# Row loads and folded steps moved to other cycles in the first pass of a two-layer graph attention kernel

## The chip, the cores and the metric

The kernel runs on one core of one Trainium2 chip. The metric is the device time of one execution in microseconds. An engine is called by its short name: PE is TensorE (the matrix engine), DVE is VectorE, ACT is ScalarE, POOL is GpSimd and SP is SyncE, which here only asks for DMA transfers. A profiled execution gives a span, from the first to the last recorded instruction, and a time of its own, which is a little longer.

## What is computed

The input `x` has 4096 rows of 512, `adj` is a 4096 x 4096 matrix of zeros and ones. Two layers follow each other, each with a residual and a layer norm. The first is graph attention with eight heads of 64 columns, and all that matters here lies in it:

```python
feats  = einsum('nf,hfo->hno', X, W)
s_self = einsum('hno,ho->hn', feats, a_self)
s_neigh = einsum('hno,ho->hn', feats, a_neigh)
dense = s_self[:, :, None] + s_neigh[:, None, :]
dense = where(dense > 0, dense, 0.2 * dense) * A[None, :, :]
out = einsum('hij,hjo->hio', softmax(dense, axis=-1), feats) + b[:, None, :]
x = layernorm(x + relu(out))
```

The second layer is attention inside 32 graphs of 128 rows, with scores that are shifted by the adjacency:

```python
a = where(mask, query @ key.T * scale, 0.0)
scores = (a + adj + adj) * where(mask, 1.0, -1000000.0)
x = layernorm(x + (softmax(scores, axis=-1) * mask) @ value)
```

## The kernel before

**Passes, chunks, steps and cycles.** The eight heads are taken in four passes `r` of two heads each. A pass goes through four chunks `c` of 1024 columns (C), and a chunk through 32 steps `j` of 128 neighbours. In passes 0 to 2 (called the first to third) eight steps make a cycle (`wide=8`), so a chunk has four cycles; in the last pass a cycle has four steps, and the second layer's work is threaded between them by a plan that is written out by hand. The instructions of PE stand in the order of the program; a scheduler orders those of the other engines, except for those that `in_order` pins to program order.

**What a step does.** The exponential of a leaky ReLU is a product of a row factor and the larger of two terms. So DVE makes, for each of the two heads, `q = max(p_row, d) * at` (L1534), in which `at` is the turned adjacency block of 128 x 1024. ACT, or DVE for one of eight, makes `mark` from q (L1544, L1539): which side of the maximum was taken. PE multiplies: `accf` gets f_s times at (L1558, four products of 512 columns a step, called the A products), `acc` gets g_s times q (L1581, eight products of 32 rows a step, which the profile counts as sixteen), and `dens` gets the marks (L1597). In the first pass `ae` also gets sums over the adjacency (L1479).

**A folded step** leaves its four A products out. DVE forms `q = (max(p_row, d) * U_row - c) * at` with two operations for each head in place of one (L1522 and L1525), and the L1581 products of that step go to `accf`. `folded(j)` says which steps of a pass do so, in the first and in the last pass only. The U rows lie in two tiles of the pool `ck`, loaded once a chunk (`rows_for_folded`, L1462), which are free again when the last folded step of the chunk before has read them.

**Where the adjacency comes from.** In the first pass POOL asks for a block of it (`load_adjacency`, L605: 1024 x 512 numbers, four steps, made fp8 on the way; the pool has three of them, `a_b`). PE turns it (`turned_steps`, L617), ACT casts it into `at` (`cast_steps`, L628), and POOL writes `at` to `at_d` in DRAM (L629), from where SP reads it back in the later passes (L635). A cycle turns the steps of the next cycle: four after the A products and four after the sums over the adjacency. They are called the first and the second turn. The request for the block of step j + 10 is pinned at the turn of j, wherever j % 4 is 2; so the block that is asked for at a second turn is used at the first turn of the next cycle but one, about a cycle and the A products later.

**The rows of a chunk.** `p_row` (two tiles of 512 KB, two buffers each) is needed from a chunk's first step on. `u_row` (two halves of 256 KB, one buffer) is needed at the end of the chunk alone, where `sums_to_rows` makes `ys = (accf + S) * u_row` and adds `acc` (L1278, L1286); what is left of that function, with `n0` and `hst` (L1306, L1312, L1362) and the write of the chunk's rows to `hs_d` (L1372), runs in the next chunk's first three cycles. [...] f_s (512 KB for four steps) and g_s (256 KB) have two buffers each, so those of the next cycle are asked for as PE finishes with those of this one.

Of the kernel before, what the change touches and what calls it, by code (L numbers as in the profile page):

```python
# [10 lines left out]
F32 = mybir.dt.float32  # L11
# [8 lines left out]
P = 128  # L20
# [378 lines left out]
def broadcast_rows(v, parts, n):  # L399

    return bass.AP(tensor=v.tensor, offset=v.offset, ap=[[0, parts], [1, n]])
# [3 lines left out]
def adjacency_streamed_path(  # L405
# [29 lines left out]
    nc = tc.nc  # L435
    N, F = x.shape
    H, _, FH = W.shape
    NT = N // P
    FC = F // P
    PR = H // 2  # L440
    FP = 2 * FH
# [3 lines left out]
    C = 1024  # L445
    CT = C // P
    NCH = N // C
# [14 lines left out]
    g_d = dram.tile([PR, NT // 4, P, 4 * FP], F32, name="g_d")  # L462
    f_d = dram.tile([PR, NT // 4, P, 4 * 2 * FP], F32, name="f_d")
    FOLDED = (0, PR - 1)
    FOLDS = {4: (1,), 5: (0, 1), 6: (0, 1, 2)}, {2: (1,), 4: (1,), 5: (0, 1), 6: (0, 1, 2)}
    HU = 2 * len(FOLDED)
    pu_d = dram.tile([2 * H + HU, N], F32, name="pu_d")
    at_d = dram.tile([NCH, NT, P, C], F32, name="at_d")
# [73 lines left out]
    rowp = ctx.enter_context(tc.tile_pool(name="rows_f", bufs=2))  # L542
    urowp = ctx.enter_context(tc.tile_pool(name="urows", bufs=1))
# [46 lines left out]
    def in_order(pinned, ins):  # L590

        if pinned:
            tc.keep_in_program_order(ins)
# [29 lines left out]
    def cast_steps(c, j, pt, steps=range(2)):  # L623

        both = pt.rearrange("p t n -> p (t n)").bitcast(FP8).rearrange("p (n k) -> p n k", k=2)
        for k in steps:
            at = ats[0, c, j + k] = ring("at", atp, 6).tile([P, C], F32R, name="at")
            ends_of_setup["ACT"] = nc.scalar.copy(at, both[:, :, k])  # L628
            nc.gpsimd.dma_start(at_d[c, j + k], at.bitcast(F32))  # L629
# [9 lines left out]
    with tc.tile_pool(name="setup1", bufs=1, side="right") as one, tc.tile_pool(  # L639
        name="setup_rows", bufs=1, side="right"  # L640
    ) as late, tc.tile_pool(name="setup2", bufs=2, side="right") as two, tc.tile_pool(
        name="xtp", bufs=4, side="right"
    ) as xtp, tc.tile_pool(name="staged1", bufs=1, side="right") as staged1, tc.tile_pool(
        name="staged2", bufs=2, side="right"
    ) as staged2, tc.tile_pool(
        name="ps_setup", bufs=3, space=PSUM
    ) as pss, tc.tile_pool(name="ps_feat", bufs=2, space=PSUM) as psf:
        NB = NT // 4
        xts, xTs, pu_js, rows = {}, {}, {}, {}
# [773 lines left out]

    steps = [(r, c, j) for r in range(PR) for c in range(NCH) for j in range(NT)]

    def main_pass(r, ae=None, wide=4):

        for c in range(NCH):
            p_row = []
            for h in range(2):  # L1430
                p_row.append(rowp.tile([P, C], F32, name=f"p_row{h}"))
                in_order(
                    r == 0 and c < 2,
                    nc.sync.dma_start(p_row[h], broadcast_rows(pu_d[2 * r + h, ts(c, C)], P, C)),
                )
            u_row = urowp.tile([P, C], F32, name="u_row")
            for h in range(2):
                in_order(
                    r == 0 and c < 2,
                    nc.sync.dma_start(  # L1440
                        u_row[h * FH : (h + 1) * FH, :],
                        broadcast_rows(pu_d[H + 2 * r + h, ts(c, C)], FH, C),
                    ),
                )
            U_row = []

            def folded(j):

                if r == PR - 1:
                    return r in FOLDED and c > 0 and j % 4 in FOLDS[c > 1].get(j // 4, ())  # L1450
                return r in FOLDED and j % 8 == 2 and (0 if c else 8) < j < NT - 8

            def rows_for_folded():

# [35 lines left out]
            for j0 in range(0, NT, wide):  # L1490
                at_step = steps.index((r, c, j0))
                cycle = range(j0, j0 + wide)
                f_s, g_s = {}, {}
                for k in range(j0 // 4, (j0 + wide) // 4):
                    f_s[k] = fsp.tile([P, 4, 2, FP], F32R, name="f_s")
                    ins = nc.sync.dma_start(
                        f_s[k].rearrange("p u s n -> p (u s n)").bitcast(F32), f_d[r, k]
                    )
                    in_order(r == 0 and c == 0 and j0 < 16, ins)
                    g_s[k] = gfp.tile([P, 4, 2, FH], F32, name="g_s")  # L1500
                    ins = nc.sync.dma_start(
                        g_s[k].rearrange("p u h o -> p (u h o)"), g_d[r, k]
                    )
                    in_order(r == 0 and c == 0 and j0 < 16, ins)
                if at_step == 0:
                    cast_steps(0, 6, last_pair)
                if any(map(folded, range(NT))) and j0 == (4 if r else 0):
                    rows_for_folded()
# [6 lines left out]
                for j in cycle:  # L1515
                    for h in range(2):
# [3 lines left out]
                        if folded(j):  # L1520
                            cn = c_all[r][:, j, h : h + 1]
                            nc.vector.scalar_tensor_tensor(  # L1522
                                q, p_row[h], d_j, U_row[h], op0=OP.max, op1=OP.mult
                            )
                            nc.vector.scalar_tensor_tensor(  # L1525
                                q, q, cn, ats[r, c, j].bitcast(F32), op0=OP.subtract, op1=OP.mult
                            )
                            mark = marks[j, h] = sgp.tile([P, C], FP8, name="mark")
                            nc.scalar.activation(  # L1529
                                mark, q, AF.Sigmoid, bias=below_0, scale=2.0**80, saturate=False  # L1530
                            )
                            continue
# [5 lines left out]
                        if j % 4 == 3 and h == 1:  # L1538
                            nc.vector.tensor_scalar(  # L1539
                                mark, q, d_j, None, op0=OP.is_gt, saturate=False  # L1540
# [14 lines left out]
                for j in cycle:  # L1555
                    for w in range(0 if folded(j) else 2):
                        for s in range(2):
                            nc.tensor.matmul(  # L1558
                                accf[:, s, :],
                                f_s[j // 4][:, j % 4, w, :],  # L1560
                                ats[r, c, j][:, ts(s, HB)],
                                start=(j == 0 and w == 0),
                                stop=(j == NT - 1 and w == 1),
                            )
# [11 lines left out]
                for j in cycle:  # L1576
                    dst = accf if folded(j) else acc
                    for s in range(2):
                        for o in range(0, FP, 32):
                            h = o // FH  # L1580
# [47 lines left out]
    with tc.tile_pool(name="ps_ae", bufs=1, space=PSUM) as psx:  # L1628
        ae = psx.tile([P, HB], F32, name="ae")
        nc.vector.memset(ae, 0.0)  # L1630
        banks.append(psx)
        main_pass(0, ae, wide=8)
        banks.remove(psx)
    first_pass.close()
    banks.extend([ctx.enter_context(tc.tile_pool(name="ps_misc2", bufs=2, space=PSUM))] * 2)
    with tc.tile_pool(name="wl1", bufs=1, side="right") as wp:
        work.append(weights_of_layer_1(keep, wp))
        work.append(kind_of_graphs(wp))
        work.append(kind_of_scores(wp))
        main_pass(1, wide=8)  # L1640
        for gen in work:
            for _ in gen:
                pass
        work.clear()
    main_pass(2, wide=8)
    more.clear()
    wide_passes.close()
    with tc.tile_pool(name="lp", bufs=2) as lp, tc.tile_pool(
        name="lp1", bufs=1
# [7 lines left out]
@with_exitstack  # L1657
def tile_gat_then_graph_attention(ctx: ExitStack, tc: tile.TileContext, *args: bass.AP):
    nc = tc.nc
    keep = ctx.enter_context(tc.tile_pool(name="flag", bufs=1))  # L1660
    flag = keep.tile([1, 1], I32, name="flag")
    adjacency_streamed_path(tc, flag, *args)
    other = nc.values_load(flag[0:1, 0:1], min_val=0, max_val=1)
    with tc.If(other > 0):
        general_path(tc, *args)
# [42 lines left out]
```

## Time and profile before

| | us |
|---|---|
| median of three runs | 2042.51 (2039.18 to 2042.93) |
| the profiled execution's own time | 2043.19 |
| its span | 2041.3 |
| PE busy | 2005.9 |
| DVE busy | 1744.8 |
| ACT busy | 1533.1 |
| first pass on PE, from the first A product | 160.2 to about 582 |

In the views below, a row of a timeline has the start in us, the duration in us, the engine, the line, the operation, what is written from what, the shape, and how many instructions were merged into it; in brackets stands how long the engine sat idle before, and what ended that. A row of SPq is a request, not the transfer. The strip called DMA has 40 equal slices of the span, each with the share of time in tenths that the DMA engines were busy.

### The profile page before, as it was taken

The page shows a single profiled execution, that of the slowest core. Times are in us where ns is not written, and L with a number is a line of the kernel's source. Part 1 is how long each engine was busy: PE and PEld are TensorE (multiplying, and loading weights), DVE is VectorE, ACT ScalarE, POOL GpSimd, SP SyncE. Part 2 cuts the span into 40 slices and gives each one's busy share as a digit, 9 for nine tenths or more (in the row PEclk, how much of TensorE's full clock was granted, in tenths as well). Part 3 has the DMA queues.
Part 4 walks back from the last instruction along what each step waited for, and adds up shares of the span by engine and source line. Part 5 has one row for each costly group of instructions (what it writes and reads, how often), then busy time and mean ns, then how long its engine had stood idle before and what let it go on. Part 6 is the DMA issues. An engine that isn't in the chain of part 4 may idle for free.

```text
span 2041.3 us, 38200 instructions
## 1 busy us (share of the span) xinstructions
PE 2005.9 (98%) x14981; PEld 1030.0 (50%) x14981; DVE 1744.8 (85%) x2219; ACT 1533.1 (75%) x1872; POOL 231.0 (11%) x362
## 2 busy tenths in 40 slices
PE   8999999999999999999999999999999999999997
PEld 7885545444444444444444544444444444445443
DVE  5668898898999998798999989999997897889754
ACT  3348988788888889788899889999786566567420
POOL 1222222222200000000000000000020210211111
PEclk9999999999999999999999999999999999999999
DMA  6899999999999999788999999989975775775211
GB/s 206 240 320 280 283 286 288 285 280 282 316 377 342 346 359 342 261 311 292 318 321 338 313 328 338 335 277 368 323 277 186 249 255 173 232 273 176 73 55 44
DMA packets 209386, 558.70 MB, mean 274 GB/s; under 512 B 25052, under 2 KB 66012, under 8 KB 209196
## 3 DMA queue, kind: packets, MB, share of 16 engines
q1 hardware_dynamic: 144844, 433.65, 61.0%
q0 software_dynamic: 62272, 121.98, 23.3%
q8 instruction: 120, 1.97, 0.4%
q10 hardware_dynamic: 2080, 0.52, 0.1%
q14 instruction: 70, 0.57, 0.1%
HBM read 499.13 MB, written 107.28 MB: 297 GB/s over the span
## 4 chain that ended last, share of the span: by engine, by line
PE 85%; DMA 7%; DVE 5%; issue 1%; ACT 1%; SPq 0%; POOL 0%; POOLq 0%; DVEq 0%; ACTq 0%
PE acc L1581 35%; PE accf L1558 20%; PE ps_fe L818 5%; PE ps_m L1186 5%; PE ps_m L1114 5%; PE dens L1597 5%; DMA a_b<-in_adj_dram 4%; DVE q L1534 3%; PE accf L1581 2%; PE ps_m L1141 1%; PE ps_m L1200 1%; DMA hp_l<-hs_d 1%; PE ps_m L617 1%; DMA at_d<-at 1%; PE ps_m L1043 1%
## 5 line engine op out<-in xcount | busy, mean ns | idle before, releaser
L1534 DVE SCALAR_TENSOR_TENSOR q<-p_row,d_all,at 128x1024 f32<-128x1024 f32 x962 | 1168.1, 1279 | 106.0 <-PE acc L1581 78.8
L1544 ACT ACTIVATE mark<-q,nb_all 128x1024 fp8e4<-128x1024 f32 x834 | 926.8, 1144 | 174.7 <-DVE q L1534 160.1
L1581 PE MATMUL acc<-q,g_s 128*32 128x512 f32 x7696 | 853.7, 594 | 1.1 <-DVE q L1534 0.4
L1581 PEld LDWEIGHTS acc<-q,g_s 128*32 128x32 f32 x7696 | 250.2, 110 | 557.2 <-issue 496.3
L1558 PE MATMUL accf<-at,f_s 128*128 128x512 f32 x1924 | 469.3, 400 | 1.7 <-ACT at L628 1.6
L1558 PEld LDWEIGHTS accf<-at,f_s 128*128 128x128 f32 x1924 | 357.2, 189 | 107.3 <-issue 27.8
L1249 ACT ACTIVATE ck<-ck,neg_half_f 128x1024 f32<-128x1024 f32 x128 | 146.0, 1141 | 28.5 <-DMA ck<-in_adj_dram 28.4
L1250 ACT ACTIVATE ck<-ck,neg_quarter 128x1024 f32<-128x1024 f32 x128 | 146.3, 1143 | 1.8
L1597 PE MATMUL dens<-mark,e_b 128*6 128x512 fp8e4 x2048 | 125.3, 379 | 2.5 <-DVE mark L1539 2.5
L818 PE MATMUL ps_fe<-w_sb_f,xT_f 128*128 128x264 f32 (+1 forms) x512 | 121.6, 395 | 1.7 <-ACT xT_f L730 1.7
L628 ACT CAST at<-ps_m 128x1024 fp32r<-128x1024 fp8e4 x124 | 116.3, 1022 | 4.8 <-issue 2.0
L1186 PE MATMUL ps_m<-wvT,x1T 128*128 128x512 f32 x256 | 114.2, 594 | 0.0
L1114 PE MATMUL ps_m<-x1T,M_sb 128*128 128x512 f32 x256 | 113.1, 595 | 0.0
L818 PEld LDWEIGHTS ps_fe<-w_sb_f,xT_f 128*128 128x128 f32 x512 | 100.5, 200 | 16.2 <-ACT xT_f L730 2.3
L1372 POOL DMA_DIRECT2D hs_d<-hst x12 | 10.7, 896 | 828.1 <-DVE hst L1362 817.5
L1539 DVE TENSOR_SCALAR mark<-q,d_all 128x1024 fp8e4<-128x1024 f32 x128 | 96.2, 751 | 4.7
L629 POOL DMA_DIRECT2D at_d<-at x128 | 69.1, 540 | 272.5 <-ACT at L628 94.0
L1597 PEld LDWEIGHTS <-e_b 128*6 128x6 bf16 x2048 | 55.9, 86 | 80.1 <-issue 38.2
L1529 ACT ACTIVATE mark<-q,below 128x1024 fp8e4<-128x1024 f32 x62 | 69.6, 1153 | 24.5 <-DVE q L1525 24.2
L1114 PEld LDWEIGHTS ps_m<-x1T,M_sb 128*128 128x128 f32 x256 | 48.0, 190 | 58.9 <-issue 57.1
L1525 DVE SCALAR_TENSOR_TENSOR q<-q,c_all,at 128x1024 f32<-128x1024 f32 x62 | 77.3, 1273 | 0.0
L1186 PEld LDWEIGHTS ps_m<-wvT,x1T 128*128 128x128 f32 x256 | 47.7, 190 | 56.3 <-issue 55.1
(207 smaller groups left out, 1294.9 us busy)
## 6 DMA issues: line engine op xcount, KB each, us to landing
at<-at_d SPq DMA_DIRECT2D x384, 512.0 KB, 6.1
f_s<-f_d SPq DMA_DIRECT2D x128, 512.0 KB, 7.8
at_d<-at POOLq DMA_DIRECT2D x128, 512.0 KB, 19.1
ck<-in_adj_dram SPq DMA_DIRECT2D x128, 512.0 KB, 5.5
g_s<-g_d SPq DMA_DIRECT2D x128, 256.0 KB, 5.9
f_d<-fst POOLq DMA_DIRECT2D x16, 1024.0 KB, 7.5
a_b<-in_adj_dram POOLq DMA_DIRECT2D x32, 512.0 KB, 21.7
p_row<-pu_d SPq DMA_DIRECT2D x32, 512.0 KB, 6.7
```

Of the source, the lines that this page charges most:

```text
L628: ends_of_setup["ACT"] = nc.scalar.copy(at, both[:, :, k])
L818: nc.tensor.matmul(pf[:, q, :, cols], tile_j(xTs[k][:, c].rearrange("p u n -> p (u n)"), u), w_sb[:, c, 4 * q : 4 * q + 4, cols], start=(c ...
L1114: nc.tensor.matmul(pz, L1["M"][:, f, ts(c, P)], x1T[:, f, :], start=(f == 0), stop=(f == FC - 1),)
L1186: nc.tensor.matmul(pv, x1T[:, f, ts(u, P)], L1["wvT"][:, f, :], start=(f == 0), stop=(f == FC - 1),)
L1249: tc.keep_in_program_order(nc.scalar.activation(ck, ck, AF.Square, bias=neg_half))
L1250: nc.scalar.activation(ck, ck, AF.Abs, bias=neg_quarter, accum_out=binp[:, k : k + 1])
L1534: ends_of_setup["Q"] = nc.vector.scalar_tensor_tensor(q, p_row[h], d_j, ats[r, c, j].bitcast(F32), op0=OP.max, op1=OP.mult)
L1539: nc.vector.tensor_scalar(mark, q, d_j, None, op0=OP.is_gt, saturate=False)
L1544: nc.scalar.activation(mark, q, AF.Sigmoid, bias=nb_all[:, j, hh : hh + 1], scale=BIG, saturate=False,)
L1558: nc.tensor.matmul(accf[:, s, :], f_s[j // 4][:, j % 4, w, :], ats[r, c, j][:, ts(s, HB)], start=(j == 0 and w == 0), stop=(j == NT - 1 an ...
L1581: nc.tensor.matmul(dst[o : o + 32, s, :], g_s[j // 4][:, j % 4, h, o % FH : o % FH + 32], qs[j, h][:, ts(s, HB)], start=(j == 0), stop=(j ...
L1597: nc.tensor.matmul(dens[lo : lo + 6, :], e_b[:, j, 2 * r + h, :], marks[j, h][:, ts(s, HB)], start=(j == 0), stop=(j == NT - 1),)
```

## The change

In the first pass the folded steps are 8, 16 and 24 of every chunk. They were 10 and 18 in chunk 0 and 2, 10 and 18 in the others. The two halves of `u_row` are asked for with a chunk's second cycle instead of its start (chunk 0 keeps it at the start), and the next chunk's `p_row` with the third cycle. Both are pinned on SP's queue. The load of `f_s` leaves out the folded steps at the two ends of its four, in both passes that fold. The table `FOLDS` is written by chunk, with the same steps as before.

```diff
-    FOLDS = {4: (1,), 5: (0, 1), 6: (0, 1, 2)}, {2: (1,), 4: (1,), 5: (0, 1), 6: (0, 1, 2)}
+    FOLDS = {1: {4: (1,), 5: (0, 1), 6: (0, 1, 2)}, 2: {2: (1,), 4: (1,), 5: (0, 1), 6: (0, 1, 2)}, 3: {2: (1,), 4: (1,), 5: (0, 1), 6: (0, 1, 2)}}
...
+    p_rows = {}
+
+    def load_p_rows(r, c, pinned):
+
+        rows = []
+        for h in range(2):
+            rows.append(rowp.tile([P, C], F32, name=f"p_row{h}"))
+            ins = nc.sync.dma_start(rows[h], broadcast_rows(pu_d[2 * r + h, ts(c, C)], P, C))
+            in_order(pinned, ins)
+        return rows
+
+    def load_u_row(r, c, pinned):
+
+        u_row = urowp.tile([P, C], F32, name="u_row")
+        for h in range(2):
+            ins = nc.sync.dma_start(
+                u_row[h * FH : (h + 1) * FH, :],
+                broadcast_rows(pu_d[H + 2 * r + h, ts(c, C)], FH, C),
+            )
+            in_order(pinned, ins)
+        return u_row
...
         for c in range(NCH):
-            p_row = []
-            for h in range(2):
-                p_row.append(rowp.tile([P, C], F32, name=f"p_row{h}"))
-                in_order(
-                    r == 0 and c < 2,
-                    nc.sync.dma_start(p_row[h], broadcast_rows(pu_d[2 * r + h, ts(c, C)], P, C)),
-                )
-            u_row = urowp.tile([P, C], F32, name="u_row")
...
+            p_row = p_rows.pop((r, c), None) or load_p_rows(r, c, (r, c) == (0, 0))
+            if r or c == 0:
+                u_row = load_u_row(r, c, r == 0)
...
-                return r in FOLDED and j % 8 == 2 and (0 if c else 8) < j < NT - 8
+                return r in FOLDED and j % 8 == 0 and j > 0
...
+                    live = [u for u in range(4) if not folded(4 * k + u)]
                     ins = nc.sync.dma_start(
-                        f_s[k].rearrange("p u s n -> p (u s n)").bitcast(F32), f_d[r, k]
+                        f_s[k][:, live[0] : live[-1] + 1].rearrange("p u s n -> p (u s n)").bitcast(F32),
+                        f_d[r, k, :, live[0] * 2 * FP : (live[-1] + 1) * 2 * FP],
                     )
...
+                if r == 0 and c and j0 == 8:
+                    u_row = load_u_row(r, c, True)
+                if r == 0 and c < NCH - 1 and j0 == 16:
+                    p_rows[r, c + 1] = load_p_rows(r, c + 1, True)
```

More of the change, by code (lines that the diff above doesn't have):

```diff
@@ L1424, in adjacency_streamed_path @@
     steps = [(r, c, j) for r in range(PR) for c in range(NCH) for j in range(NT)]
+    p_rows = {}
[15 more added lines that the diff above has]
+        return u_row
     def main_pass(r, ae=None, wide=4):
         for c in range(NCH):
-            p_row = []
-            for h in range(2):
-                p_row.append(rowp.tile([P, C], F32, name=f"p_row{h}"))
-                in_order(
-                    r == 0 and c < 2,
-                    nc.sync.dma_start(p_row[h], broadcast_rows(pu_d[2 * r + h, ts(c, C)], P, C)),
-                )
-            u_row = urowp.tile([P, C], F32, name="u_row")
[L1437 to L1444, printed above, removed]
+            p_row = p_rows.pop((r, c), None) or load_p_rows(r, c, (r, c) == (0, 0))
+            if r or c == 0:
+                u_row = load_u_row(r, c, r == 0)
             U_row = []
@@ L1449, in folded @@
                 if r == PR - 1:
-                    return r in FOLDED and c > 0 and j % 4 in FOLDS[c > 1].get(j // 4, ())
-                return r in FOLDED and j % 8 == 2 and (0 if c else 8) < j < NT - 8
+                    return r in FOLDED and c > 0 and j % 4 in FOLDS[c].get(j // 4, ())
+                return r in FOLDED and j % 8 == 0 and j > 0
             def rows_for_folded():
```

## The prediction

> **What bounds the kernel now.** I read the page's busy times first, then TensorE's timeline over the first pass, then what stands behind each of its gaps on the queues.
>
> ```profile
> PE 2005.9 (98%) x14981; PEld 1030.0 (50%) x14981; DVE 1744.8 (85%) x2219; ACT 1533.1 (75%) x1872; POOL 231.0 (11%) x362
> DMA  6899999999999999788999999989975775775211
> ```
>
> TensorE is busy 98% of the span; slices 3 to 16 (100 to 810 us) also have every DMA engine busy 90% or more. The first pass runs from 160.2 to 582 us. A cycle of eight steps there is: A products into accf, first turn (L617), 128 products into acc, dens, ae, second turn. Without a wait A takes 6.5 us to the next turn with one folded step and 7.4 without. The timeline at three starts of a chunk:
>
> ```profile
> 264.86 6.97 PE L1558 MATMUL accf<-at,f_s 128*128 128x512 f32 x28
> 272.24 1.07 PE L617 MATMUL ps_m<-ident_b,a_b 128*128 128x128 bf16 x16 [0.41 <-DMA a_b<-in_adj_dram]
> ...
> 369.24 7.01 PE L1558 MATMUL accf<-at,f_s 128*128 128x512 f32 x28
> 379.89 1.07 PE L617 MATMUL ps_m<-ident_b,a_b 128*128 128x128 bf16 x16 [3.63 <-DMA a_b<-in_adj_dram]
> 380.88 5.31 PE L1581 MATMUL acc<-q,g_s 128*32 128x512 f32 x32
> ...
> 478.58 7.00 PE L1558 MATMUL accf<-at,f_s 128*128 128x512 f32 x28
> 487.78 1.07 PE L617 MATMUL ps_m<-ident_b,a_b 128*128 128x128 bf16 x16 [2.19 <-DMA a_b<-in_adj_dram]
> 488.78 3.64 PE L1581 MATMUL acc<-q,g_s 128*32 128x512 f32 x32
> ```
>
> From the start of A to the turn are 7.38, 10.65 and 9.20 us; less 6.53 that is 0.85, 4.12 and 2.67, together **7.64 us** of waiting for a block of the adjacency. After the longest, 32 products take 5.31 instead of 3.64: 1.67 us more. So **9.3 us** lie at three starts. A wait of L617 for DVE later in each of these cycles (0.35 to 0.37 us shown) is left alone by the change.
>
> The late block is the one that POOL asks for at 352.91. Its row in POOL's timeline, and SP's rows just then:
>
> ```profile
> 348.51 0.91 POOL L1372 DMA_DIRECT2D hs_d<-hst  x1 [5.27 <-DVE q L1534]
> 352.91 0.90 POOL L605 DMA_DIRECT2D a_b<-in_adj_dram  x1 [1.17 <-DMA at_d<-at]
> ```
> ```profile
> 352.38 1.09 SPq L1440 DMA_DIRECT2D u_row<-pu_d  x2
> 362.38 1.51 SPq L1434 DMA_DIRECT2D p_row<-pu_d  x2
> ```
>
> It lands 26.9 us later; those of 244.15 and 461.25 take 28.0 and 26.5; elsewhere it is 17.9 to 25.4. All three share their flight with u_row (2 x 256 KB) and p_row (2 x 512 KB). POOL's writes at_d take 17 to 25 us to land (medians of the DMA view, cycle by cycle): its queue has a standing backlog.
>
> [...] the three blocks in flight with SP's rows are the slowest. [...] the DMA view of 552 to 576 us has 408 GB/s, which I use. [...] Here 3.63 us idle cost 1.67 us and 2.19 us cost nothing[...].
>
> **The change, part by part.** A cycle's DMA work, with a_b counted as read (four bytes for each written), is 8 x 0.524 for at_d, 2 x 2.10 for a_b and 1.57 MB for f_s and g_s: 9.96 MB, or 24.4 us at 408 GB/s, beside 25 to 26 us of TensorE. Row loads (p, u, and U rows in ck: 2.62 MB) and hs_d (0.52) add 7.7 us to a chunk. An estimate: 105 us of DMA, where chunk 1 took TensorE 104.4 (264.86 to 369.24) with 0.85 of waiting. DMA and TensorE are level, and DMA falls behind where rows bunch.
>
> 1. Folded steps: 12 for 11. Per chunk they were 2, 3, 3, 3 and are 3 each, now at steps 8, 16 and 24. One more fold takes four A products away; A's two lengths in the timeline (7.58 and 6.68) give 0.9 us: **-0.9 us**, on the path. It costs DVE two operations, 2.5 us, in chunk 0's last cycle; in chunk 1's DVE waited 2.16 and 1.54 us there (<-PE), so it is free. If that cover were gone, up to +2.5.
> 2. The folds leave the first cycle, where DVE also has the chunk's two ys operations (1.28 and 1.22). DVE loses 2.5 us there and gains it in the fourth cycle, which had none. In DVE's order as many operations stand ahead of n0 (L1306) and hst (L1362) as before, so hs_d is asked for no later. On the path: 0.
> 3. Rows. SP asked at a chunk's start for u and the next-but-one p; now u is asked for with the second cycle and the next p with the third. U rows (ck) wait for the last fold and move from the start of the third cycle to its end. u and p are used long after they land (a whole cycle and more), so their own lateness costs 0. On SP the second g_s load of a first cycle no longer stands behind u_row, which waited for ys; a g_s of the fourth cycle now stands behind a ck that waits for DVE's fold, but is needed a cycle later: 0.
> 4. f_s of a block with a folded step 0 is 384 KB, not 512: twelve times in the first pass, 1.57 MB. In the last pass six loads shrink to 256 or 128 KB (three each, 1.97 MB); no wait of TensorE there names f_s, so 0, with half a microsecond either way.
> 5. What rows and f_s give back. DMA never idles from 185 us to the third wait, so a block lands earlier by the work no longer ahead of it. Ahead of each late block one u and one p set are gone (1.57 MB, 3.9 us), and 3, 6 and 9 smaller f_s (0.39, 0.79, 1.18 MB: 1.0, 1.9, 2.9 us): 4.8, 5.8 and 6.7 us. Without waits TensorE would arrive 0.85, 4.97 and 9.3 us earlier (the last with the clock). The first two waits go wholly; at the third, the block is 6.7 us earlier and TensorE could be 9.3, so about 2.6 us of waiting stays: **-6.7 us**. Counting only what is in flight with the block (1.57 MB becomes 1.05 MB of ck, with smaller f_s, 1.6 us a block) gives 0.85 + 1.6 + 1.67 + 1.6 = 5.7. Both ends: 0 (waits move) to 9.3 (all gone). I take 6.7.
> 6. ACT's order changes, which the diff doesn't show: the two marks of a folded step now stand ahead of the four casts (L628) that follow the second turn, and one cast after the first turn stands behind some five marks. In the third cycle of chunk 1 the casts ended 0.6 us before A reached their steps; with DVE's last operation of the fold where a q now ends (343.2), its mark ending at 344.4 and casts 0.95 us apart I get 0.8 us. Cost 0 to +1.4 a cycle (two marks of 1.15 less 0.85); I take 0.
>
> Sum: -0.9 - 6.7 = **-7.6 us**. The profiled execution took 2043.19 us (span 2041.3), so **2035.6**; that execution is 0.7 above the median of 2042.51. Passes 2 to 4 have almost no TensorE waits and should only start earlier. POOL's order is the same.
>
> **Rivals.** *Waits that move (0.24).* p now comes in the third cycle and ck at its end, 2.1 MB just ahead of the very block that was late, whose issue already waits for at_d landings. Then it is no earlier, and only the first wait, the fold and part of the clock come back: 0.9 + 0.85 + 1 = 2.8, about 2040.4. For it: POOL's wait of 1.17 above, and at_d landings of 20 to 25 us after ck loads. Against: 1.57 MB net is gone from ahead of it. *Casts late (0.11, slower).* Place: ACT, after the second turn of each cycle. If DVE's second operation of the fold ends over 0.8 us later than I have it, A waits for at; at the bound of 1.4 us in 12 cycles, 17 us are lost against 7.6 gained: 2052. It turns slower than before from 0.63 us a cycle. *All waits gone (inside the forecast, less likely):* 10.2 us, 2033. *The change doing less than it says:* the built order of SP shows u, p and f_s where I have them, so I give it nothing of its own.
>
> **How the numbers follow.** The forecast (gains of 5 to 10.5) has 0.65, moved waits 0.24, late casts 0.11. About 0.2% (4.1 us) is what a measurement of this kernel can tell from no change. Faster by more: 0.65 and a little of the second case, less gains that fall short: 0.66. Within: 0.23. Slower: 0.11. The forecast's own range is 2032 to 2038; to hold 8 in 10 it reaches over moved waits to 2042, and half a microsecond below for runs under the median.
>
> **What would show it.** Right: L617 at the starts of chunks 1 and 2 without a wait for a_b, under 3 us at chunk 3; no 5.31 after it; a_b landings there of 20 to 24 us; TensorE reaching the second pass 7 to 8 us earlier, and no more gained after it. Wrong: a_b waits of the old size there or new ones inside a chunk (rows); waits of A for ACT's at (casts); a changed time between 582 us and the end.

## The result, and the profile after

| | before | after |
|---|---|---|
| median, us | 2041.64 (12 runs, 2037.71 to 2045.53) | 2035.55 (12 runs, 2030.43 to 2039.35) |
| ratio after / before | | 0.9969, interval 0.9959 to 0.998 |
| profiled execution's own time | 2043.19 | 2035.39 |
| its span | 2041.3 | 2033.6 |
| first pass on TensorE, first A product to the first of the second pass | 422.8 (160.17 to 582.97) | 414.7 (158.71 to 573.43) |

By the ratio the kernel is 6.3 us faster (2.0 to 4.1 parts in a thousand, so 4 to 8 us), by the two medians 6.1; the forecast was 7.6 us faster and 2035.6. A second comparison of the same two kernels, later, gave 0.9964 (0.995 to 0.9977).

The lines of the page of after that answer to those shown of before, the busy times and the strip of the DMA engines in 40 slices:

```profile
PE 2005.0 (99%) x14977; PEld 1027.5 (51%) x14977; DVE 1746.3 (86%) x2221; ACT 1523.3 (75%) x1872; POOL 231.3 (11%) x362
DMA  6999999999999999798999999979976775775211
```

They hardly move: TensorE 99% instead of 98%, the DMA engines still at 9 through the whole first pass. The whole change is in what these lines can't show, the waits. TensorE's timeline of after at the same three starts of a chunk (start, duration, engine, line, operation, shape, count; a wait would stand in brackets):

```profile
262.85 7.57 PE L1573 MATMUL accf<-at,f_s 128*128 128x512 f32 x32
270.26 1.07 PE L617 MATMUL ps_m<-ident_b,a_b 128*128 128x128 bf16 x16
...
367.00 7.60 PE L1573 MATMUL accf<-at,f_s 128*128 128x512 f32 x32
374.44 1.07 PE L617 MATMUL ps_m<-ident_b,a_b 128*128 128x128 bf16 x16
...
471.07 7.56 PE L1573 MATMUL accf<-at,f_s 128*128 128x512 f32 x32
478.54 1.07 PE L617 MATMUL ps_m<-ident_b,a_b 128*128 128x128 bf16 x16
479.54 5.79 PE L1596 MATMUL acc<-q,g_s 128*32 128x512 f32 x52
```

32 A products stand where 28 stood (no folded step in the first cycle any more), and none of the three first turns waits for a block. From the start of A to the turn it is 7.41, 7.44 and 7.47 us, the plain length of 32 products. After the third, 52 products take 5.79 us; the clock granted from 479.5 to 485.3 us is 1.00. The list of waits has the same news in one line each. Before, then after (what waited, for what: us in all, times, the longest):

```profile
PE ps_m L617 <- DMA a_b<-in_adj_dram: 6.2, 3, 3.6
...
PE accf L1558 <- ACT at L628: 1.6, 1, 1.6
```

```profile
PE accf L1573 <- ACT at L628: 2.2, 4, 1.6
```

The first line is gone. The second has grown from one wait to four: the long one, at the start of the pass, is in both, and A now waits for ACT's casts three times more, about 0.2 us each. POOL's timeline of after around the block that was latest before, and SP's requests ahead of it:

```profile
344.46 0.91 POOL L1372 DMA_DIRECT2D hs_d<-hst  x1 [7.28 <-DMA a_b<-in_adj_dram]
346.63 0.54 POOL L629 DMA_DIRECT2D at_d<-at  x1 [1.26 <-ACT at L628]
347.90 0.53 POOL L629 DMA_DIRECT2D at_d<-at  x1 [0.72 <-ACT at L628]
349.18 0.90 POOL L605 DMA_DIRECT2D a_b<-in_adj_dram  x1 [0.75 <-PE accf L1573]
```

```profile
285.63 2.41 SPq L1441 DMA_DIRECT2D u_row<-pu_d  x2
...
311.83 2.61 SPq L1433 DMA_DIRECT2D p_row<-pu_d  x2
...
336.02 0.32 SPq L1471 DMA_DIRECT2D ck<-pu_d  x1
...
339.08 0.32 SPq L1471 DMA_DIRECT2D ck<-pu_d  x1
```

The last rows of u and p ahead of the request at 349.18 were asked for 64 and 37 us before it; the U rows alone stand just ahead. Request and landing of the three late blocks, and the turn that needs each:

| block | before | after | turn of after | in hand |
|---|---|---|---|---|
| chunk 1 | 244.2 + 28.0 | 244.1 + 20.9 | 270.26 | 5.3 |
| chunk 2 | 352.9 + 26.9 | 349.2 + 21.0 | 374.44 | 4.2 |
| chunk 3 | 461.2 + 26.5 | 455.5 + 23.0 | 478.54 | 0.0 |

The last column shrinks from chunk to chunk. DMA is still the slower of the two; the pass ends about when nothing is left in hand.

A single profile scatters outside the first pass: over the kernels run here its start lies between 157.2 and 160.9 us, and what follows it took 1455.3 to 1460.5 us. Before has 160.2 and 1458.3, after 158.7 and 1460.2. So the comparison of two profiles below is made by the length of the first pass, and the comparison of times by medians.

### The profile page after: what moved, and what is told of

The parts are those of the page before. It is cut to its first block, busy times and chain, and to the rows that moved or that the text cites. A ratio compares the mean times of both kernels' runs of the same rounds, so it can differ in the third digit from the quotient of the medians.

```text
span 2033.6 us, 38136 instructions
## 1 busy us (share of the span) xinstructions
PE 2005.0 (99%) x14977; PEld 1027.5 (51%) x14977; DVE 1746.3 (86%) x2221; ACT 1523.3 (75%) x1872; POOL 231.3 (11%) x362
## 5 line engine op out<-in xcount | busy, mean ns | idle before, releaser
L1559 ACT ACTIVATE mark<-q,nb_all 128x1024 fp8e4<-128x1024 f32 x832 | 915.2, 1148 | 140.9 <-DVE q L1549 130.3
```

Of the source, the lines that this page charges most:

```text
L1559: nc.scalar.activation(mark, q, AF.Sigmoid, bias=nb_all[:, j, hh : hh + 1], scale=BIG, saturate=False,)
```

## The experiments

Twelve kernels ran, four at a time, each beside runs of before (medians 2039.8, 2040.4 and 2040.44). Two things had to be told apart: whether the gain comes from DMA work that no longer stands ahead of the late blocks, and which part of the change brings it: the rows, the folds or f_s. "Pass" is the length of the first pass in the one profiled execution.

**1. Rows alone** (`rows_only`: after, with the folds and the f_s of before).

```diff
-                return r in FOLDED and j % 8 == 0 and j > 0
+                return r in FOLDED and j % 8 == 2 and (0 if c else 8) < j < NT - 8
...
-                        f_s[k][:, live[0] : live[-1] + 1].rearrange("p u s n -> p (u s n)").bitcast(F32),
-                        f_d[r, k, :, live[0] * 2 * FP : (live[-1] + 1) * 2 * FP],
+                        f_s[k].rearrange("p u s n -> p (u s n)").bitcast(F32), f_d[r, k]
```

> The u and p requests in the second and third cycle, with the folded steps and the f_s loads of before. Theory (a late block lands earlier by all the DMA work that no longer stands ahead of it): 1.57 MB less ahead of each late block, 3.9 us at 408 GB/s; the wait at chunk 1 (0.85 us) goes, at chunk 2 about 1 us stays and the slow clock after it goes, at chunk 3 some 3 to 4 us in all stay; 3 to 5 us faster than before. Rival (the waits go because DVE has no fold at a chunk's start): the three waits for a_b stay within 1 us of 0.85, 4.12 and 2.67, and the time is that of before.

Measured: ratio 1.0001 (0.9992 to 1.001), pass 419.4. Its timeline has no wait at chunks 1 and 2 and this at chunk 3:

```profile
471.37 7.01 PE L1571 MATMUL accf<-at,f_s 128*128 128x512 f32 x28
481.57 1.54 PE L617 MATMUL ps_m<-ident_b,a_b 128*128 128x128 bf16 x16 [3.19 <-DMA a_b<-in_adj_dram]
483.04 4.79 PE L1594 MATMUL acc<-q,g_s 128*32 128x512 f32 x32
```

The first two waits are gone, as step 5 of the prediction has it, but at chunk 3 a longer one than before is left: 3.19 us, and the products after it are slower (4.79 us where 3.64 is usual). The expected 3 to 5 us did not come: moving the rows alone gives nothing that the times can tell.

**2. Folds alone** (`folds_only`: before, with the folds of after).

```diff
-                return r in FOLDED and j % 8 == 2 and (0 if c else 8) < j < NT - 8
+                return r in FOLDED and j % 8 == 0 and j > 0
```

> Folded steps 8, 16 and 24 of each chunk, with the row requests at the chunk's start and full f_s loads as before. Theory: one more fold gives 0.9 us, DVE's share of the first cycle wins nothing, the three waits for a_b stay (7 to 10 us with the slow clock, perhaps more, since the U rows now come just ahead of u and p): 0 to 1 us faster, or up to 3 us slower. Rival (DVE at the chunk's start): the waits go and it is 8 to 10 us faster.

Measured: 1.0004 (0.9997 to 1.0011), pass 422.0. The waits of its first two chunk starts, in its timeline:

```profile
270.05 1.07 PE L617 MATMUL ps_m<-ident_b,a_b 128*128 128x128 bf16 x16 [0.96 <-DMA a_b<-in_adj_dram]
...
377.95 1.89 PE L617 MATMUL ps_m<-ident_b,a_b 128*128 128x128 bf16 x16 [3.64 <-DMA a_b<-in_adj_dram]
```

The late blocks are as late as before (241.0 + 29.0, 350.6 + 27.3). Chunk 3 had no wait here: the cycle with the wait at chunk 2 took 33.4 us, where 27.0 is its length without one, so TensorE came 6.4 us later to what follows.

**3. All but the smaller f_s** (`full_f`: after, with f_s whole as in experiment 1).

> The changed kernel with every f_s load of 512 KB. Theory: 0.39, 0.79 and 1.18 MB more stand ahead of the three late blocks, 1.0, 1.9 and 2.9 us; in the changed kernel these land about 5.3, 4.2 and 0.0 us ahead of the turn that needs them, so only the third turn waits, by about 2.9 us: 2 to 3 us slower than the changed kernel, 4.5 to 5.5 us faster than before. Rival (only what is in flight with the block counts, 0.13 to 0.26 MB): under 0.7 us, so 7 to 8 us faster than before.

Measured: 0.9978 (0.9971 to 0.9984), pass 415.4. One wait for a block is left, at chunk 3:

```profile
479.65 1.07 PE L617 MATMUL ps_m<-ident_b,a_b 128*128 128x128 bf16 x16 [0.76 <-DMA a_b<-in_adj_dram]
```

So rows and folds together bring 4.5 us, though neither brings any alone. Without the smaller f_s the block of chunk 3 lands at 479.6 instead of 478.5. About 2.9 us of waiting were expected there, and under 0.7 by the rival; the 0.76 stand by the rival.

**4. p one cycle later** (`p_fourth`).

```diff
-                if r == 0 and c < NCH - 1 and j0 == 16:
+                if r == 0 and c < NCH - 1 and j0 == 24:
```

> The changed kernel with the next chunk's p asked for with the fourth cycle instead of the third: the same work ahead of the late block, but now in flight with it. Theory (all work ahead counts): the same landings and the same time as the changed kernel, within 1 us. Rival (what is in flight counts): the late blocks take 2.6 us longer to land (1.05 MB), and with 5.3, 4.2 and 0.0 us in hand the turn at chunk 3 waits about 2.6 us.

Measured: 0.9978 (0.9972 to 0.9985), pass 415.3. p is again in flight with the late blocks, which take 22.9, 24.6 and 26.5 us to land for 20.9, 21.0 and 23.0 of after, and still TensorE waits only 0.36 us at chunk 3:

```profile
481.16 1.07 PE L617 MATMUL ps_m<-ident_b,a_b 128*128 128x128 bf16 x16 [0.36 <-DMA a_b<-in_adj_dram]
```

The rival had 2.6 us. At chunks 1 and 2 the time in hand takes the slower landing up. At chunk 3, where there is none, the block was asked for earlier: 18.6 us ahead of the chunk's first A product for 15.6 in after. So work counts that lies ahead of a block, whether it flies with the block or delays its request.

**5. Folds in the third step of a cycle** (`fold_26`: full_f, with folds 10, 18 and 26). It is meant to take the casts' lateness away and nothing else.

```diff
-                return r in FOLDED and j % 8 == 0 and j > 0
+                return r in FOLDED and j % 8 == 2 and j > 8
```

> Rows asked for as in the changed kernel, full f_s loads, folded steps 10, 18 and 26 of every chunk: out of a chunk's first cycle, but third in their cycle, so that ACT's marks stand behind the four casts after the second turn as before. Two theories. If what counts is that the first cycle has no fold (its first turn then comes 0.9 us later, 7.4 instead of 6.5 us after the first A product, and DVE has less to do there), this is as good as the changed kernel with full f_s (4.5 us faster than before) or better, and the A products lose their 0.1 to 0.5 us a cycle of waiting for casts: 5 to 8 us faster than before. If the folded step must be first in its cycle, it is like the rows alone: within 2 us of before.

Measured: 0.9988 (0.9981 to 0.9995), pass 420.2. A no longer waits for casts (fourth cycles 24.9 us instead of 25.3 to 25.4), but blocks are late again, one of them at a third cycle. Its timeline at both places:

```profile
427.44 1.07 PE L617 MATMUL ps_m<-ident_b,a_b 128*128 128x128 bf16 x16 [2.47 <-DMA a_b<-in_adj_dram]
428.44 3.64 PE L1594 MATMUL acc<-q,g_s 128*32 128x512 f32 x32
...
483.07 1.21 PE L617 MATMUL ps_m<-ident_b,a_b 128*128 128x128 bf16 x16 [3.64 <-DMA a_b<-in_adj_dram]
484.20 6.00 PE L1594 MATMUL acc<-q,g_s 128*32 128x512 f32 x40
```

TensorE's own work is shorter here than in full_f, and the kernel isn't faster (its median stands 2.6 us below before, full_f's 4.9, in different sets of runs). The expected 5 to 8 us did not come. In this profile the two waits cost 8.2 us where TensorE's own work is 2 us shorter, and the execution lies 2.4 us over its kernel's median; the intervals of the two ratios overlap. So the waits can come back here; that they always cost what the shorter work gains is not shown.

**6. Folds in the fifth step** (`fold4`: after, with folds 12, 20 and 28).

```diff
-                return r in FOLDED and j % 8 == 0 and j > 0
+                return r in FOLDED and j % 8 == 4 and j > 4
```

> The changed kernel with folded steps 12, 20 and 28: the fifth of their cycle, in the second half of it, f_s loads still shrunk (its last three steps). The casts that A waited for now have four whole steps of A products before them, so the waits of A for at should go (about 2 us over the pass): 6 to 9 us faster than before. Rival: the fold now falls into the acc products, where DVE is only just ahead of TensorE (2.5 us for a step's two q against 1.73), so acc waits 1 to 2.5 us in each of 12 cycles: 10 us slower than that or more.

Measured: 1.0078 (1.0065 to 1.0092), pass 437.3. No block is late; cycles are 27.0 to 28.1 us instead of 25.3 to 27.1. Its groups on TensorE's weight loads, and its DVE timeline at a chunk's first fold:

```profile
L1596 PEld LDWEIGHTS acc<-q,g_s 128*32 128x32 f32 x900 | 29.9, 109 | 72.6 <-issue 51.0 <-DVE q L1549 18.9 <-DVE q L1537 1.8
```

```profile
360.72 2.48 DVE L1537 SCALAR_TENSOR_TENSOR q<-p_row,d_all,ck 128x1024 f32<-128x1024 f32 x2 [2.97 <-PE acc L1596]
363.12 2.47 DVE L1540 SCALAR_TENSOR_TENSOR q<-q,c_all,at 128x1024 f32<-128x1024 f32 x2
```

In the stretch from 265 to 480 us those loads wait 20.7 us for a q of DVE; in after it is 4.8. DVE first stands idle until products of acc are done, then has four operations to do where two are usual, and q is late. With TensorE about 2 us slower in all cycles but a chunk's first, every block lands more than 11 us ahead of its turn. So the place of a fold within its cycle decides over some 16 us against before.

**7. No rows** (`no_rows`: before, with p and u loaded in chunk 0 alone in the first pass).

```diff
-            p_row = []
-            for h in range(2):
+            if r or c == 0:
+                p_row = []
+            for h in range(2) if r or c == 0 else ():
...
-            u_row = urowp.tile([P, C], F32, name="u_row")
-            for h in range(2):
+            if r or c == 0:
+                u_row = urowp.tile([P, C], F32, name="u_row")
+            for h in range(2) if r or c == 0 else ():
```

> The kernel before, with u_row and p_row of the first pass loaded for chunk 0 alone and used for all its chunks, so the results of chunks 1 to 3 in that pass are of the wrong rows; folds and f_s as before. It takes 1.57 MB of loads out of each chunk. Theory (DMA work ahead of the blocks): all three waits for a_b go, 6 to 9 us faster than before, although the folds stay in the first cycle. Rival (the folds in the first cycle hold the block back by way of DVE, ACT and POOL): waits of over 2 us stay at chunks 2 and 3.

Measured: 0.9967 (0.9955 to 0.9979), pass 413.9. Folds and f_s are those of before, yet the waits for blocks are all gone. Its timeline at chunk 3:

```profile
471.86 6.99 PE L1560 MATMUL accf<-at,f_s 128*128 128x512 f32 x28
478.69 1.07 PE L617 MATMUL ps_m<-ident_b,a_b 128*128 128x128 bf16 x16
```

This is the clearest run for the mechanism: take DMA work away from ahead of the late blocks, change nothing on TensorE, and the whole of the waits comes back. It takes the rows away where the change only moves them, so here DMA is the faster of the two: 6.9, 9.2 and 12.4 us are in hand at the three turns, where in after the time in hand shrinks. It also shows the length of a first cycle with a fold and no wait: 26.4 us, with 6.80 to 6.85 us from A to the turn.

**8. p loaded twice** (`p_twice`: after, with a second load of the same rows into the same tiles), and **9. f rows in its place** (`f_twice`: 1.05 MB a chunk read from f_d, plain rows, ahead of p).

```diff
...
+                    for h in range(2):
+                        ins = nc.sync.dma_start(
+                            p_rows[r, c + 1][h],
+                            broadcast_rows(pu_d[2 * r + h, ts(c + 1, C)], P, C),
+                        )
+                        in_order(True, ins)
```

```diff
...
+                        in_order(True, nc.sync.dma_start(rows[h], f_d[r, 2 + h]))
...
```

> The changed kernel with each p_row load of chunks 1 to 3 in the first pass done twice (1.05 MB more a chunk, in the third cycle). Theory (work ahead counts, and DMA has no spare time): 2.6, 5.1 and 7.7 us later landings at the three late blocks against 5.3, 4.2 and 0.0 us in hand: about 0, 1 and 7 us of waiting, in all 7 us slower than the changed kernel, so about as slow as before. Rival (DMA catches up within a chunk): 2.6 us later at each: a wait at chunk 3 alone, 2 to 3 us.

> The changed kernel with 1.05 MB a chunk added in the third cycle as in the run with p twice, but read from f_d, where every partition reads 4 KB of its own, and not from one row that all 128 read (the p rows are loaded over it). If bytes are what counts, the same waits as there: about 3.3 us at the fourth cycle of chunks 1 and 2, and 5 to 6 us slower than the changed kernel. If a row read by all partitions costs DMA more than its bytes, the waits are under 1.5 us and it is 1 to 3 us slower.

Measured: p_twice 1.001 (1.0003 to 1.0016), pass 423.3; f_twice 1.0001 (0.9993 to 1.0009), pass 422.8. Each gives the whole gain away. The new waits of p_twice, then of f_twice, in their timelines:

```profile
349.73 1.89 PE L617 MATMUL ps_m<-ident_b,a_b 128*128 128x128 bf16 x16 [2.61 <-DMA a_b<-in_adj_dram]
...
457.92 1.30 PE L617 MATMUL ps_m<-ident_b,a_b 128*128 128x128 bf16 x16 [2.54 <-DMA a_b<-in_adj_dram]
```

```profile
352.39 1.07 PE L617 MATMUL ps_m<-ident_b,a_b 128*128 128x128 bf16 x16 [1.47 <-DMA a_b<-in_adj_dram]
...
460.42 1.89 PE L617 MATMUL ps_m<-ident_b,a_b 128*128 128x128 bf16 x16 [3.74 <-DMA a_b<-in_adj_dram]
```

They lie a cycle earlier than those of before, at the fourth cycle's turn, for the block that is in flight with the doubled load (28.3 us to land in both chunks of p_twice, 28.5 and 27.0 in f_twice). The expectations had them there for f_twice, and at the late blocks for p_twice. So 1.05 MB a chunk is all that stands between waits and none. Plain rows cost about as much as broadcast ones (5.2 us of waits in each): as far as two runs tell, it is the bytes.

**10. Folds in the fourth step** (`fold_27`: after, with folds 11, 19 and 27), and **11. the same with the second pass's first p deferred too** (`fold_27_p`).

```diff
-                return r in FOLDED and j % 8 == 0 and j > 0
+                return r in FOLDED and j % 8 == 3 and j > 8
```

```diff
-                if r == 0 and c < NCH - 1 and j0 == 16:
-                    p_rows[r, c + 1] = load_p_rows(r, c + 1, True)
+                if r == 0 and j0 == 16:
+                    after_c = (r, c + 1) if c < NCH - 1 else (r + 1, 0)
+                    p_rows[after_c] = load_p_rows(*after_c, True)
```

> The changed kernel with folded steps 11, 19 and 27: fourth in their cycle, so the casts after the second turn stand ahead of the fold's marks, and still at the end of their four steps, so that f_s loads stay shrunk. The A products should no longer wait for casts (about 2 to 3 us over the pass). Theory (the DMA engines set the pace, so time that TensorE wins turns into waits for a_b): the waits come back at chunk 3 or inside a chunk, smaller than with 10, 18 and 26 and full f_s, since 1.18 MB less is ahead; the time is within 2 us of the changed kernel. Rival (the casts' delay is simply lost): 2 to 3 us faster than the changed kernel.

> As the one with folds 11, 19 and 27, and the second pass's first p_row (1.05 MB) is asked for with chunk 3's third cycle instead of its first, so that it no longer flies with the last late block. Theory: the block of chunk 3 lands 2.6 us earlier and what was left of its wait goes, by up to 2.6 us; 0 to 3 us faster than without, and 1 to 4 us faster than the changed kernel.

Measured: 0.9965 (0.9951 to 0.9979) and 0.9971 (0.9959 to 0.9983), the same as after within the intervals. The waits of A for casts, which were to go, are still there (0.15 to 0.22 us). fold_27's profiled execution had one wait, 3.31 us at chunk 3, and a pass of 421.1; its median tells that this is not its rule. fold_27_p had none, 415.1, with the block of chunk 3 landing at 477.2. The 1 to 4 us that the deferred p was to bring did not come: no version here is clearly better than the change itself.

**12. The change once more** (`changed_again`).

> The changed kernel itself, beside the others on one chip: 4 to 8 us faster than before, no wait for a_b over 1 us in the first pass.

Measured: 0.9964 (0.995 to 0.9977), pass 414.8, every cycle within 0.1 us of the first profile of after, no wait for a block. In hand at the three turns are 5.9, 4.7 and 0.9 us. So a second profile shows what the first one showed.

## Why the prediction was right, and where not

The time came out as forecast, and the mechanism is the one given: DMA work ahead of the blocks made them late. But the sum came out by two errors that cancel, so that it came this close was in part luck. Cycle by cycle (start of A to start of A), chunks 1 to 3:

| | first | second | third | fourth |
|---|---|---|---|---|
| before | 27.0, 31.9, 28.8 | 25.6 | 26.0 | 25.8, 25.8, 24.0 |
| no_rows | 26.4 | 25.6 | 26.0 | 25.8, 25.8, 24.0 |
| after | 27.0, 27.0, 27.1 | 25.7, 25.6, 25.6 | 26.1 | 25.4, 25.4, 23.6 |
| fold_26 | 27.0, 27.0, 32.5 | 25.6 | 26.0 (28.7 once) | 24.9, 24.9, 23.1 |

- **What there was to win (step 5).** Against no_rows the three first cycles of before hold 0.6 + 5.5 + 2.4 = 8.5 us. The prediction had 9.3, since it took 6.53 us as the length from A to the turn; at a chunk's start it is 6.83 without any wait.
- **What came back (step 5).** It had 6.7 with some 2.6 us left at chunk 3. All of the 8.5 came back. The rows alone leave 3.19 us at chunk 3, all but f_s 0.76, the whole change 0. The step failed in holding that the 4.8 to 6.7 us of transfers decide alone. The place of the folds, which step 2 had costed at nothing, matters to the same block: full_f differs from rows_only in it alone and waits 2.43 us less at chunk 3. Of that 0.6 us are that A is longer with the fold out of the first cycle (7.44 for 6.83), so that the turn comes later just where the block is late. The other 1.9 are that the block landed earlier (479.6 for 481.5), though both had moved as much by then (119.5 and 119.6 MB since chunk 0's second cycle); why is open. In fold_26, with the same first cycle, the block landed at 483.0, so the longer A is not all.
- **The folds (steps 1, 2 and 6).** Forecast: -0.9, 0 and 0. Measured: in each of chunks 1 to 3, +0.6 in the first cycle, up to +0.1 in the second and third, -0.4 in the fourth; in chunk 0, +0.4 in the third and -0.5 in the fourth. Together +0.8, the difference between the passes of after (414.7) and no_rows (413.9), neither of which has a wait for a block. The error lies for the most part in step 6: a cycle with late casts takes 25.3 or 25.4 us where fold_26, with the fold two steps later, takes 24.9. In the third cycle of chunk 0 and the four fourth cycles that is some 2.3 us, between the 0 taken and the bound of 1.4 us a cycle.
- **Sum.** -8.5 + 0.8, and 0.4 less in chunk 0's first cycle, which has no part in the change, are the 8.1 us between the two passes; the forecast's terms were -6.7 and -0.9.
- **f_s (step 4 and its part of 5).** 2.9 us of transfers ahead of the third block were forecast to make it as much earlier; between full_f and after it lands 1.1 us earlier (1.4 in changed_again), and TensorE waits 0.76 us less. That is all the traces show of it; the ratios, 0.9978 without it and 0.9969 and 0.9964 with it, are 2 to 3 us apart, but their intervals overlap.
- **Rows (step 3)** are never waited for, as forecast. No wait of TensorE names them. SP asks for them one behind the other with its other loads: in after, two requests for g_s stand from 278.42 to 285.58 us, and u_row follows at 285.63.

The rivals. *Waits that move* is what rows_only and fold_26 show: there a wait taken away at one place came up at another. In after it didn't, because rows, folds and f_s were moved together. *Casts late* is real and small, 2.3 us and not 17. Removing it did not pay in fold_26, where waits for DMA came in its place, in two lumps (2.47 and 3.64 us), and after the longer one 128 products took 15.44 us instead of 13.94; that the one brings the other is argued from one profile.

The prediction's account of DMA and TensorE as level holds. Counted by the bytes of the DMA view, with a_b as read, before moved 76.86 MB in the 190.8 us from chunk 0's second cycle to its second late block, 403 GB/s; after came to 406, rows_only 405, no_rows 408. The rate changes little from kernel to kernel, what is ahead of a block changes more; but one part in a hundred of it is 2 us of such a stretch, so differences of 1 or 2 us between single landings are within what it scatters.

One more thing shows in POOL's own waits. In before, from 160 to 560 us, it stood idle before 37 of its writes of at_d and 13 of its requests for a block until an earlier at_d had landed, 50.2 us in all and 2.0 at the longest; in after it was 27 and 12, with 40.0 us and 2.2. So in these two what slows those landings also puts off some requests for a block. What makes POOL wait for them is not shown.

Open: rows_only's profiled pass is 3.4 us shorter than that of before, while its median is not. Waits vary from one execution to the next (fold_27's profile is such a case), and the profiled execution of before lies 1.5 us over its median, but its other executions were not traced.

## What to carry to other kernels

Where DMA and the limiting engine are level, busy shares tell nothing (TensorE 98% before and 99% after, here): lay the landing of each buffered load beside the instruction that needs it and follow the time in hand from stage to stage. Transfers that nobody needs soon go to where the most is in hand, and the part that is taken away and the deadline that is moved have to be judged together, since either alone may give nothing (rows_only 1.0001, folds_only 1.0004). A small regular delay on an engine that would otherwise wait for DMA may cost less than it seems (the late casts took 2.3 us): with it taken away, long waits can be back, as fold_26 had them (2.47 and 3.64 us).

## What the runs showed of the hardware

A wait can cost more than its length. The table has every wait for a block over 1 us, with the excess of its cycle over the same cycle without a wait. The last two columns are the length of the turn that ended the wait (1.07 us is usual) and that of the 16, 32 or 128 products after it, with their usual length in brackets.

| wait shown, us | kernel | cycle | without it | cost | turn | products after it |
|---|---|---|---|---|---|---|
| 1.47 | f_twice | 27.0 | 25.4 | 1.6 | 1.07 | 1.92 (1.92) |
| 2.19 | before | 28.8 | 26.4 | 2.4 | 1.07 | 3.64 (3.64) |
| 2.47 | fold_26 | 28.7 | 26.0 | 2.7 | 1.07 | 3.64 (3.64) |
| 2.54 | p_twice | 29.7 | 25.4 | 4.3 | 1.30 | 3.32 (1.92) |
| 2.61 | p_twice | 29.6 | 25.4 | 4.2 | 1.89 | 2.51 (1.92) |
| 3.19 | rows_only | 31.4 | 26.4 | 5.0 | 1.54 | 4.79 (3.64) |
| 3.31 | fold_27 | 33.0 | 27.0 | 6.0 | 1.89 | 15.96 (13.94) |
| 3.63 | before | 31.9 | 26.4 | 5.5 | 1.07 | 5.31 (3.64) |
| 3.64 | folds_only | 33.4 | 27.0 | 6.4 | 1.89 | 15.68 (13.94) |
| 3.64 | fold_26 | 32.5 | 27.0 | 5.5 | 1.21 | 15.44 (13.94) |
| 3.74 | f_twice | 31.9 | 25.4 | 6.5 | 1.89 | 3.64 (1.92) |

The first three waits cost themselves and at most 0.2 us more. The other eight cost 1.6 to 2.8 us more, and most of that is in the turn and the products just after them. In before the granted clock was 0.50 from 381 to 384 us, after the wait of 3.63 us, and 1.00 again from 385 to 388; around the wait of 2.19 us, from 487 to 493, it stayed at 1.00. The length of a wait alone does not order what it costs: 3.31 us cost 2.7 more, 3.63 us 1.9 more. What decides it is not shown by these waits.
